# Layer 2 of a graph network: transposes alternating with the turned sums, and one product for both transposed halves

## The chip, the cores and the metric

The kernel runs on one core of a Trainium2 chip. A core has four compute engines used here: TensorE (PE, matrix products and transposes into PSUM; its weight loads are listed apart as PEld), VectorE (DVE), ScalarE (ACT) and GpSimd (POOL). Each works through its own queue in order, and semaphores make one wait for another. SyncE (SP) issues the loads from memory.

The metric is the device time of one execution in microseconds. The times before are 1147.15, 1148.13 and 1155.05 us, median 1148.13. The profile is of one execution, whose span from the first to the last instruction is 1148.0 us.

## What is computed

Four graph layers over the same 4096 nodes with 64 features and one sparse, weighted adjacency matrix of 4096 x 4096. Each layer normalizes x, works on it and adds its result to x. Layer 0 is a plain neighbour sum, layer 1 an attention with sigmoid weights, layer 3 weights each row's last 100 neighbours by powers of a half. The change is in layer 2, which sums logarithmic maps of all neighbours on the Poincare ball:

```python
def _logmap(x, y, c):
    sub = _mobius_add(-x, y, c)
    sub_norm = jnp.maximum(jnp.linalg.norm(sub, axis=-1, keepdims=True), MIN_NORM)
    ...
    arg = jnp.clip(sqrt_c * sub_norm, 0.0, TANH_CLIP)
    return 2.0 / (sqrt_c * lam_x) * jnp.arctanh(arg) * sub / sub_norm
...
deg = jnp.maximum(adj.sum(axis=1, keepdims=True), 1e-08)
w = adj / deg
log_ij = _logmap(x[:, None, :], x[None, :, :], c)
agg = jnp.einsum('ij,ijc->ic', w, log_ij)
transformed = agg @ weight + bias
origin = jnp.zeros_like(transformed)
return _expmap(origin, transformed, c)
```

So every pair of nodes gets a factor (an arctanh of a distance over its norm), the factor is multiplied by the adjacency, and the products weight a sum over source nodes. The factor of a pair is the same in both directions; the adjacency is not.

## The kernel before

**Blocks and groups.** Targets come in 8 blocks of 512 (`ib`), sources in groups of 256 (`g`, two column chunks of 128, `G = 2`). Layer 2 walks over `work`, a list of 72 entries `d`: block `ib` against the groups of the source blocks `J >= ib`, two groups (`half` 0 and 1) a block. Since the factor is symmetric, only `J >= ib` is computed. Where `J > ib` (`d["two"]`, 56 entries), the factors are used twice: as they are, for the targets of block `ib`, and transposed, for the targets of block `J`. On the diagonal there are a `first` entry, whose lower part is transposed once, and a `cut` entry.

**The steps of an entry.** Distances: fp32 and bf16 matmuls into a PSUM tile `mm` of 128x1024 (`l2_dists`, `l2_signs`). Then by turns ACT, POOL and DVE on 128x1024: `v<-mm` square on ACT, `v<-v` clamp on POOL (partly on DVE), logarithm `v<-v,minus` and root `t<-v` on ACT, `t<-mm,t` on DVE (`l2_coshs`), logarithm `t<-t` and inverse root `v<-v` on ACT, and `t<-t,v` on DVE (`l2_pairs`). The last is called the pairing here; `t` then holds the factors. From there two ways lead on:

- plain: DVE multiplies `t` by the adjacency tile (`l2_weights`, `w<-t,adj`), and PE sums with the sources' features `HA` as weights (`l2_sums`, `acc<-w,HA` with 512 moving columns, 65 weight columns);
- turned, for `two` only: PE transposes the eight 128x128 pieces of `t` into two PSUM banks, one per half `c` (`l2_turns`, `tr<-ident,t`); DVE multiplies each bank by the adjacency of the other direction (`l2_weights2`, `w<-tr,adj`, two instructions of 128x512) into `w2`; PE sums `w2` over its four chunks (`l2_sums2`, `acc<-w,HA` with 256 columns) into the accumulator `acc1`. After the second half of a source block, DVE (ACT for block 0) adds that accumulator to `others`, which frees it (`l2_gathers`).

An fp32 matmul shows as two passes in the trace, each with its own weight load, a transpose as one.

**What sets the order.** The order of each engine's queue is laid down when the program is built. Each stage is a generator that yields an engine and a time from which its next piece could run; `in_turn` always takes the piece that a small model (`Pace`) thinks can start first. `in_steps` ties generators to steps: in step k, PE issues the distances of entry k+1, the signs of entry k, the turned sums of entry k-2, the transposes of entry k-1, and the plain sums of entry k-1:

```python
(l2_dists(), -1, once), (l2_signs(), 0, once), (l2_sums2(), 2, if_two(1)),
(l2_turns(), 1, lambda d: 2 if d["two"] else 1), (l2_sums(), 1, once),
```

The two PSUM banks for transposes, `tr0` and `tr1`, are handed out by `bank()` from the list `spare` and given back by `emptied()`. They also serve the tail work of a finished block: `follow` queues generators such as `after2` (evicts the sums into `e`, transposes it, finishes the layer for the block) and `before3` (prepares layer 3). That work runs beside the next block's first steps. Where the model sees PE wait over 0.6 us, `keep_warm` puts in matmuls of the identity with itself (`tr<-ident`).

Of the kernel before, what the change touches and what calls it, by code (L numbers as in the profile page):

```python
# [9 lines left out]
F32 = mybir.dt.float32  # L10
# [6 lines left out]
PSUM = bass.MemoryType.PSUM  # L17

P = 128
D = 64  # L20
N = 4096
NC = N // P
W = 512
NB = N // W
CB = W // P
G = 2
# [36 lines left out]
class Pace:  # L63
# [11 lines left out]

    @staticmethod
    def name(ap):
        return getattr(getattr(ap, "tensor", ap), "name", None)

    def cost(self, engine, op, out, ins, rest, kw):  # L80
        n = per_partition(out)
# [61 lines left out]
def kernel(ctx: ExitStack, tc: tile.TileContext, a: dict, out: bass.AP):  # L143
# [4 lines left out]
    pace = Pace()  # L148
    PE, DVE, ACT, POOL = (
        InOrder(tc, e, pace, name)  # L150
        for e, name in (
            (nc.tensor, "PE"), (nc.vector, "DVE"), (nc.scalar, "ACT"), (nc.gpsimd, "POOL"),
        )
    )
# [5 lines left out]
    rows = ctx.enter_context(tc.tile_pool(name="rows", bufs=2))  # L160
    ps_mm = ctx.enter_context(tc.tile_pool(name="ps_mm", bufs=2, space=PSUM))
    ps_acc = ctx.enter_context(tc.tile_pool(name="ps_acc", bufs=1, space=PSUM))
    ps_tr = ctx.enter_context(tc.tile_pool(name="ps_tr", bufs=2, space=PSUM))


    x = keep.tile([P, NC, D], F32, name="x")
# [174 lines left out]
    in_use = []  # L341
    spare = [0, 1]

    def bank():
        k = spare.pop(0)
        t = ps_tr.tile([P, W], F32, tag=f"tr{k}", name="tr", bufs=1)
        in_use.append((t, k))
        return t

    def emptied(t):  # L350
        k = [k for k in in_use if k[0] is t][0]
        in_use.remove(k)
        spare.append(k[1])
# [379 lines left out]
    def latest(*times):  # L733
        return None if None in times else max(times)
# [86 lines left out]
    def ready(t, more=0.0):  # L821
        return pace.ready[pace.name(t)] + more
# [229 lines left out]
    def l2_dists():  # L1052
        for d in work:
            yield "PE", lambda: latest(
                l1[-1].get("dist"), rows_at.get((2, d["J"])), pair_tiles[-2].get("read")
            )
            pair_tile(d)
            ps = part(d, d["ps"])
            for c in range(G):
                b = slice(c * D, (c + 1) * D)  # L1060
                PE.matmul(
                    ps[:, c, :], LT[b, d["g"], :], RT[b, targets(d)], start=True, stop=False
                )
            for c in range(G):
                b = slice(2 * c * Q, (2 * c + 1) * Q)
                PE.matmul(
                    ps[:, c, :], LB[b, d["g"], :], RB[b, targets(d)], start=False, stop=True
                )
            d["dist"] = pace.latest
# [18 lines left out]
    def l2_clamps_v():  # L1088

        for d in work:  # L1090
            yield "DVE", lambda: d.get("square")
            if d["shared"]:
                v = d["v"].rearrange("p c i -> p (c i)")[:, 0:CLAMPED]
                DVE.tensor_scalar(v, v, FLOOR, None, ALU.max)
            d["clamped_v"] = pace.latest

    def l2_signs():
        for d in work:
            yield "PE", lambda: d.get("square")
            for c in range(G):  # L1100
                b = slice((2 * c + 1) * Q, (2 * c + 1) * Q + 2)
                PE.matmul(
                    part(d, d["ps"])[:, c, :], LB[b, d["g"], :], RB[b, targets(d)],
                    start=False, stop=True, skip_group_check=True,
                )
            d["signed"] = pace.latest
# [26 lines left out]
    def l2_coshs():  # L1133
        for d in work:
            yield "DVE", lambda: latest(d.get("root"), d.get("signed"))
            t = part(d, d["t"])
            DVE.scalar_tensor_tensor(t, part(d, d["ps"]), 0.5 * SC, t, ALU.max, ALU.add)
            d["read"] = pace.latest
# [22 lines left out]
            d["weighed"] = pace.latest  # L1161
            used(d)

    def l2_turns():
        for d in work:
            for c in range(G if d["two"] else 0):
                yield "PE", lambda: d.get("paired") if spare else None
                d["tr", c] = ps = bank()
                for k in range(CB):
                    b = slice(k * P, (k + 1) * P)  # L1170
                    PE.transpose(ps[:, b], d["t"][:, c, b], ident)
            if d["first"]:
                yield "PE", lambda: d.get("paired") if spare else None
                d["tr", 0] = ps = bank()
                for k in range(CB):
                    b, c = slice(OWN + k // G * P, OWN + (k // G + 1) * P), k % G
                    PE.transpose(ps[:, k * P : (k + 1) * P], d["t"][:, c, b], ident)
            d["turned"] = pace.latest
            if d["cut"]:
                yield "ANY", lambda: d.get("paired")  # L1180
                d["turned"] = d["paired"]
# [15 lines left out]
    def l2_weights2():  # L1197
        k = -1
        for n, d in enumerate(work):
            if d["first"]:  # L1200
                own = work[n + 1]
                yield "DVE", lambda: latest(
                    ready(d["tr", 0]) if ("tr", 0) in d else None, arrival(own),
                    ago(work, n + 1, 2, "summed"),
                )
                own["w"] = w2["pool"].tile([P, G, W], F32, tag="w", name="w")
                DVE.tensor_mul(
                    own["w"][:, :, 0:OWN], d["tr", 0].rearrange("p (k j) -> p k j", j=OWN),
                    own["adj"][:, :, 0:OWN],
                )  # L1210
                emptied(d["tr", 0])
                used(own)
            k += d["two"]
            for c in range(G if d["two"] else 0):
                yield "DVE", lambda: latest(
                    ready(d["tr", c]) if ("tr", c) in d else None,
                    ready(d["adj2"]) if "adj2" in d else None, ago(twos, k, 2, "summed2"),
                )
                if c == 0:
                    d["w2"] = w2["pool"].tile([P, CB, G * P], F32, tag="w2", name="w2")  # L1220
                j = (d["half"] * G + c) * P
                DVE.tensor_mul(
                    d["w2"][:, :, c * P : (c + 1) * P],
                    d["tr", c].rearrange("p (k j) -> p k j", j=P), d["adj2"][:, :, j : j + P],
                )
                emptied(d["tr", c])
            d["weighed2"] = pace.latest

    def l2_sums():
        for d in work:  # L1230
            yield "PE", lambda: latest(d.get("weighed"), take(0, d))
            if d["first"]:
                accs["l2"] = ps_acc.tile([P, W], F32, tag="acc0", name="acc")
                st["acc_free"][0] = None
            acc = accs["l2"]
            for c in range(G):
                PE.matmul(
                    acc[0 : D + 1, :], HA[:, d["g"] * G + c, :], d["w"][:, c, :],
                    start=(d["first"] and c == 0), stop=(d["last"] and c == G - 1),
                )  # L1240
            d["summed"] = pace.latest
            if d["last"]:
                ib = d["ib"]
                others = w2["others"][:, ws(ib)] if ib else None
                follow(
                    with_mark(3, ib, after2(ib, acc, others, st), before3(ib, None)),
                    ON_V if ib else ON_S, evicts=True,
                )

    def l2_sums2():  # L1250
        for d in twos:
            yield "PE", lambda: latest(
                d.get("weighed2"), 0.0 if d["half"] else st["acc_free"][1]
            )
            if d["half"] == 0:
                accs["turned"] = ps_acc.tile([P, W], F32, tag="acc1", name="acc")
                st["acc_free"][1] = None
            acc = accs["turned"][0 : D + 1, :]
            part = slice(d["half"] * G * P, (d["half"] + 1) * G * P)
            for k in range(CB):  # L1260
                PE.matmul(
                    acc[:, part], HA[:, d["ib"] * CB + k, :], d["w2"][:, k, :],
                    start=(k == 0), stop=(k == CB - 1),
                )
            d["summed2"] = pace.latest

    def l2_gathers():
        for d in twos:
# [25 lines left out]
    def if_two(n):  # L1294
        return lambda d: n if d["two"] else 0
# [174 lines left out]
    def l3_sum():  # L1470
# [22 lines left out]
        if d["last"]:  # L1493
# [5 lines left out]
        feed(order, "early"), feed(order23, "second"), second_tables(), second_part(), third_part(), l2_loads2(),  # L1499
        l0_sums(), l1_sums(), l1_weights(), l1_sigmoids(), l1_atts(),  # L1500
        in_steps(
            (l2_dists(), -1, once), (l2_signs(), 0, once), (l2_sums2(), 2, if_two(1)),
            (l2_turns(), 1, lambda d: 2 if d["two"] else 1), (l2_sums(), 1, once),
        ),
        in_steps(
            (l2_first_logs(), 0, once), (l2_roots(), 0, once), (l2_squares(), -1, once), (l2_inverses(), 0, once), (l2_logs(), 0, once),
# [1 line left out]
        l3_counts(),  # L1508
        in_steps(
            (l2_pairs(), 1, once), (l2_weights(), 1, once),  # L1510
            (l2_coshs(), 0, once), (l2_clamps_v(), -1, once), (l2_weights2(), 1, lambda d: 2 if d["two"] else 1 if d["first"] else 0),
        ),
        l2_clamps(), l2_gathers(), l3_weights(), l3_pass(), l3_masks(), l3_bias(),
        degree_sums(0, l0), degree_sums(1, l1), constants(), *later_constants(),
# [46 lines left out]
```

## Time and profile before

| | before |
|---|---|
| runs, us | 1147.15, 1148.13, 1155.05 |
| profiled execution, span, us | 1148.0 |
| mean granted TensorE clock | 0.990 |
| layer 2, about | 485 to 945 us of the span |
| `acc<-w,HA`, 256 columns, 500 to 900 us | 432 passes, 385 ns each |
| `tr<-ident,t` 128x128, 500 to 900 us | 456 transposes, 273 ns each |
| `w<-tr,adj` 128x512 | 120, 683 ns each |
| `t<-mm,t` 128x1024, 540 to 860 us | 48, 1220 ns each |

Nearly every instruction is recorded through one helper, so all have line L135 and are told apart by their tiles, as out<-in. Times are microseconds from the start of the span unless marked ns. Matmuls are pipelined: the 273 ns of a transpose is its whole way, while the next may start earlier, so for PE the distance from start to start counts. `xN` counts instructions (passes) in a merged line. "[0.30 <-DVE w]" behind a line means that the engine was idle for 0.30 us before it, and that DVE's write of `w` ended that. In the chain of waits every piece of work is followed back to what released it; what lies on it sets the end.

### The profile page before, as it was taken

How to read it: one execution, taken by the hardware profiler on the slowest of the kernel's cores; microseconds unless marked ns; L12 is line 12 of the kernel's file. 1: busy time of each engine (PE TensorE's matmuls, PEld its weight loads, DVE VectorE, ACT ScalarE, POOL GpSimd, SP SyncE). 2: the span in 40 equal slices, each digit the busy share in tenths (PEclk: the TensorE clock that was granted, in tenths of full speed). 3: DMA queues.
4: the chain of work that ended last, by engine and by line, in shares of the span. 5: the costliest groups of instructions: out<-in, count | busy, mean ns of one | idle time of the engine just before them, and what ended most of it. 6: DMA issues, size and time to landing. Idle time of an engine off the chain costs nothing.

```text
span 1148.0 us, 16026 instructions
## 1 busy us (share of the span) xinstructions
PE 1084.0 (94%) x5564; PEld 460.5 (40%) x5564; DVE 925.0 (81%) x1505; ACT 787.4 (69%) x1287; POOL 260.2 (23%) x150
## 2 busy tenths in 40 slices
PE   6889999999999999999999999999999879999998
PEld 3234443333333333345445445445444433333332
DVE  7689989869988888688989989899999994555550
ACT  1154546676776667889989889897988665555554
POOL 3021322112000000153343343343434300000000
PEclk9899999999999999999999999999999999999999
DMA  8899999865787677534535535435355499888930
GB/s 299 342 408 389 408 385 344 290 234 192 235 258 247 219 245 237 186 129 150 192 135 168 199 116 196 167 131 198 119 212 166 147 384 350 319 319 297 338 111 10
DMA packets 77194, 271.80 MB, mean 237 GB/s; under 512 B 10040, under 2 KB 11064, under 8 KB 77112
## 3 DMA queue, kind: packets, MB, share of 16 engines
q1 hardware_dynamic: 75456, 270.57, 65.9%
q8 instruction: 44, 0.72, 0.3%
q10 hardware_dynamic: 1656, 0.20, 0.1%
q14 instruction: 38, 0.31, 0.1%
HBM read 269.68 MB, written 1.05 MB: 236 GB/s over the span
## 4 chain that ended last, share of the span: by engine, by line
PE 51%; DVE 17%; issue 11%; ACT 9%; DMA 6%; POOL 6%; ACTq 0%; POOLq 0%; SPq 0%; DVEq 0%
PE acc L135 24%; PE mm L135 16%; PE tr L135 11%; DMA adj<-in_adjT_dram 5%; POOL v L135 5%; ACT wt L135 3%; DVE dg L135 3%; DVE sig L135 3%; DVE w L135 2%; DVE t L135 2%; ACT t L135 1%; ACT v L135 1%; ACT sig L135 1%; ACT lo_sq L135 1%; POOL lo_s L135 1%
## 5 line engine op out<-in xcount | busy, mean ns | idle before, releaser
L135 PE MATMUL acc<-w,HA 128*65 128x256 f32 (+1 forms) x736 | 246.1, 469 | 10.2 <-DVE w L135 10.0
L135 POOL TENSOR_SCALAR v<-v 128x1024 f32<-128x1024 f32 (+1 forms) x72 | 171.6, 2383 | 263.0 <-ACT v L135 263.0
L135 ACT ACTIVATE sig<-mm,att_b,att_a 128x1024 f32<-128x1024 f32 x128 | 148.6, 1201 | 51.0 <-PE mm L135 50.6
L135 ACT ACTIVATE wt<-mm 128x1024 uint16<-128x1024 f32 x124 | 120.2, 1020 | 87.2 <-PE mm L135 87.2
L135 DVE TENSOR_TENSOR sig<-sig,adj 128x1024 f32<-128x1024 f32 x128 | 152.6, 1220 | 30.0 <-ACT sig L135 26.7
L135 DVE TENSOR_TENSOR dg<-dg,adj 128x1024 f32<-128x1024 f32 x113 | 137.6, 1221 | 6.5 <-DMA adj<-in_adjT_dram 4.9
L135 PE MATMUL acc<-adj,HA 128*64 128x512 f32 x512 | 124.6, 615 | 13.0 <-DMA adj<-in_adjT_dram 12.6
L135 PEld LDWEIGHTS acc<-w,HA 128*65 128x65 f32 x736 | 94.1, 138 | 94.2 <-issue 50.0
L135 PE MATMUL mm<-qT,kT 64*128 64x512 f32 x512 | 129.2, 621 | 2.8 <-ACT sig L135 2.0
L135 PE MATMUL acc<-sig,HL 128*64 128x512 f32 x512 | 124.8, 608 | 1.7 <-DVE sig L135 1.5
L135 PE MATMUL acc<-wt,S 128*64 128x512 bf16 x496 | 100.0, 390 | 0.2 <-ACT wt L135 0.2
L135 ACT ACTIVATE v<-v,minus 128x1024 f32<-128x1024 f32 x72 | 79.1, 1099 | 29.8 <-POOL v L135 27.7
L135 DVE SCALAR_TENSOR_TENSOR t<-mm,t 128x1024 f32<-128x1024 f32 x72 | 83.5, 1160 | 13.6 <-PE mm L135 11.0
L135 DVE SCALAR_TENSOR_TENSOR t<-t,v 128x1024 f32<-128x1024 f32 x72 | 83.3, 1157 | 3.3 <-ACT t L135 2.7
L135 DVE TENSOR_TENSOR w<-t,adj 128x1024 f32<-128x1024 f32 x72 | 83.5, 1160 | 1.4
L135 DVE TENSOR_SCALAR RT<-adj 128x1024 bf16<-128x1024 f32 x74 | 50.4, 695 | 41.1 <-PE mm L135 39.9
L135 DVE TENSOR_TENSOR w<-tr,adj 128x512 f32<-128x512 f32 x120 | 77.5, 683 | 7.3 <-PE tr L135 7.2
L135 ACT ACTIVATE v<-mm 128x1024 f32<-128x1024 f32 x72 | 69.6, 967 | 14.4 <-PE mm L135 14.4
L135 ACT ACTIVATE t<-t 128x1024 f32<-128x1024 f32 x72 | 72.2, 1003 | 9.1 <-DVE t L135 9.0
L135 PE MATMUL mm<-RT,LT 64*128 64x512 f32 (+1 forms) x288 | 78.4, 621 | 0.0
L135 ACT ACTIVATE t<-v 128x1024 f32<-128x1024 f32 x72 | 72.7, 1010 | 2.1
L135 PEld LDWEIGHTS mm<-qT,kT 64*128 64x128 f32 x512 | 43.7, 186 | 71.1 <-issue 35.6
(215 smaller groups left out, 1411.3 us busy)
## 6 DMA issues: line engine op xcount, KB each, us to landing
adj<-in_adjT_dram SPq DMA_DIRECT2D x512, 512.0 KB, 4.7
x<-in_x_dram SPq DMA_DIRECT2D x4, 256.0 KB, 3.8
out_dram<-h SPq DMA_DIRECT2D x8, 128.0 KB, 2.5
b<-in_b_dram ACTq DMA_DIRECT2D x2, 32.0 KB, 5.6
W<-in_W_dram ACTq DMA_DIRECT2D x3, 16.0 KB, 4.8
W0T<-in_W0T_dram ACTq DMA_DIRECT2D x2, 16.0 KB, 5.5
W1T<-in_W1T_dram ACTq DMA_DIRECT2D x1, 16.0 KB
W1T<-in_b_dram ACTq DMA_DIRECT2D x1, 0.2 KB
```

Source lines behind the costliest of these rows:

```text
L135: done = self.tc.keep_in_program_order(getattr(self.engine, op)(*args, **kw))
```

## The change

`l2_turns` and `l2_sums2` become one generator, `l2_turns_and_sums2`. For entry n of `work` it issues the transposes of entry n and the turned sums of entry n-1 in two parts, one per half `c`. In a part, four turned matmuls (now 128 columns wide, for half `c` alone) and four transposes alternate one by one. A part starts when the pairing of entry n is done, bank `c` is spare, and `w2` of entry n-1 is ready (`weighed2`); the first part of a source block also needs `acc1` free. At ends of runs, where only one of the two kinds exists, the part holds that kind alone.

The two banks become one tile `trs` of two banks, allocated once, and bank `c` holds half `c` of a `two` entry; other users take the first spare one. `l2_weights2` then multiplies both halves in one instruction of 128x1024 when both are there, and gives both banks back behind it.

In the program as built, 224 turned matmuls of 256 columns become 448 of 128, 112 products `w<-tr,adj` become 56, and the count of `keep_warm` matmuls goes from 62 to 69 (in layer 2's blocks from the second on, from 7 together to 5 and, two steps later, 2). ScalarE's, POOL's and SyncE's instructions are the same in number.

```diff
-    ps_tr = ctx.enter_context(tc.tile_pool(name="ps_tr", bufs=2, space=PSUM))
+    ps_tr = ctx.enter_context(tc.tile_pool(name="ps_tr", bufs=1, space=PSUM))
+    trs = ps_tr.tile([P, 2, W], F32, name="tr")
...
-    def bank():
-        k = spare.pop(0)
-        t = ps_tr.tile([P, W], F32, tag=f"tr{k}", name="tr", bufs=1)
+    def bank(k=None):
+        k = spare[0] if k is None else k
+        spare.remove(k)
+        t = trs[:, k, :]
...
+    def turns_of(d):
+
+        for c in range(G if d["two"] else 1 if d["first"] else 0):
+            def start(c=c):
+                d["tr", c] = bank(c if d["two"] else None)
+
+            def one(k, c=c):
+                if d["two"]:
+                    src = d["t"][:, c, k * P : (k + 1) * P]
+                else:
+                    src = d["t"][:, k % G, OWN + k // G * P : OWN + (k // G + 1) * P]
+                PE.transpose(d["tr", c][:, k * P : (k + 1) * P], src, ident)
+
+            yield start, one
+
+    def sums2_of(d):
+
+        for c in range(G if d["two"] else 0):
+            def start(c=c):
+                if d["half"] == c == 0:
+                    accs["turned"] = ps_acc.tile([P, W], F32, tag="acc1", name="acc")
+                    st["acc_free"][1] = None
+
+            def one(k, c=c):
+                to = (d["half"] * G + c) * P
+                PE.matmul(
+                    accs["turned"][0 : D + 1, to : to + P], HA[:, d["ib"] * CB + k, :],
+                    d["w2"][:, k, c * P : (c + 1) * P], start=(k == 0), stop=(k == CB - 1),
+                    skip_group_check=True,
+                )
+
+            yield start, one
+
+    def steps_of(n):
+
+        turns = list(turns_of(work[n]))
+        sums2 = list(sums2_of(work[n - 1])) if n else []
+        return [(sums2[c : c + 1], turns[c : c + 1]) for c in range(max(len(turns), len(sums2)))]
+
+    def l2_turns_and_sums2():
+        for n, d in enumerate(work):
+            parts = steps_of(n)
+            old = work[n - 1] if n else None
+            for c, (sum2, turn) in enumerate(parts):
+                yield "PE", lambda: latest(
+                    *([d.get("paired") if (c in spare if d["two"] else spare) else None] if turn else []),
+                    *([old.get("weighed2"), 0.0 if c or old["half"] else st["acc_free"][1]] if sum2 else []),
+                    0.0,
+                )
+                for start, _ in sum2 + turn:
+                    start()
                 for k in range(CB):
...
+                    for _, one in sum2 + turn:
+                        one(k)
...
-            for c in range(G if d["two"] else 0):
+            if d["two"]:
                 yield "DVE", lambda: latest(
...
-                    d["w2"][:, :, c * P : (c + 1) * P],
-                    d["tr", c].rearrange("p (k j) -> p k j", j=P), d["adj2"][:, :, j : j + P],
-                )
-                emptied(d["tr", c])
+                    d["w2"].rearrange("p k (c j) -> p c k j", j=P),
+                    trs.rearrange("p c (k j) -> p c k j", j=P),
+                    d["adj2"][:, :, j : j + G * P].rearrange("p k (c j) -> p c k j", j=P),
+                )
+                for c in range(G):
+                    emptied(d["tr", c])
...
-            (l2_dists(), -1, once), (l2_signs(), 0, once), (l2_sums2(), 2, if_two(1)),
-            (l2_turns(), 1, lambda d: 2 if d["two"] else 1), (l2_sums(), 1, once),
+            (l2_dists(), -1, once), (l2_signs(), 0, once), 
+            (l2_turns_and_sums2(), 1, lambda d: len(steps_of(work.index(d))) + d["cut"]), (l2_sums(), 1, once),
```

More of the change, by code (lines that the diff above doesn't have):

```diff
@@ L77, in name @@
     def name(ap):
-        return getattr(getattr(ap, "tensor", ap), "name", None)
+        name = getattr(getattr(ap, "tensor", ap), "name", None)
+        if name is not None and name.startswith("tr_"):
+            return f"{name}_{ap.offset % (2 * W) // W}"
+        return name
     def cost(self, engine, op, out, ins, rest, kw):
@@ L1162, in l2_weights @@
             used(d)
-    def l2_turns():
-        for d in work:
-            for c in range(G if d["two"] else 0):
-                yield "PE", lambda: d.get("paired") if spare else None
-                d["tr", c] = ps = bank()
-                for k in range(CB):
[L1170 to L1177, printed above, removed]
+    def turns_of(d):
[9 more added lines that the diff above has]
+            yield start, one
@@ new lines, in steps_of @@
+    def steps_of(n):
[14 more added lines that the diff above has]
+                    start()
+                for k in range(CB):
+                    for _, one in sum2 + turn:
+                        one(k)
+            if old is not None and old["two"]:
+                old["summed2"] = pace.latest
@@ L1213, in l2_weights2 @@
             k += d["two"]
-            for c in range(G if d["two"] else 0):
+            if d["two"]:
                 yield "DVE", lambda: latest(
-                    ready(d["tr", c]) if ("tr", c) in d else None,
+                    *(ready(d["tr", c]) if ("tr", c) in d else None for c in range(G)),
                     ready(d["adj2"]) if "adj2" in d else None, ago(twos, k, 2, "summed2"),
                 )
-                if c == 0:
-                    d["w2"] = w2["pool"].tile([P, CB, G * P], F32, tag="w2", name="w2")
-                j = (d["half"] * G + c) * P
+                d["w2"] = w2["pool"].tile([P, CB, G * P], F32, tag="w2", name="w2")
+                j = d["half"] * G * P
                 DVE.tensor_mul(
-                    d["w2"][:, :, c * P : (c + 1) * P],
-                    d["tr", c].rearrange("p (k j) -> p k j", j=P), d["adj2"][:, :, j : j + P],
-                )
-                emptied(d["tr", c])
+                    d["w2"].rearrange("p k (c j) -> p c k j", j=P),
+                    trs.rearrange("p c (k j) -> p c k j", j=P),
+                    d["adj2"][:, :, j : j + G * P].rearrange("p k (c j) -> p c k j", j=P),
+                )
+                for c in range(G):
+                    emptied(d["tr", c])
             d["weighed2"] = pace.latest
@@ L1248, in l2_sums @@
                 )
[L1250 to L1253, printed above, removed]
-            )
[L1255 to L1265, printed above, removed]
     def l2_gathers():
@@ L1510 @@
             (l2_pairs(), 1, once), (l2_weights(), 1, once),
-            (l2_coshs(), 0, once), (l2_clamps_v(), -1, once), (l2_weights2(), 1, lambda d: 2 if d["two"] else 1 if d["first"] else 0),
+            (l2_coshs(), 0, once), (l2_clamps_v(), -1, once), (l2_weights2(), 1, lambda d: 1 if d["two"] or d["first"] else 0),
         ),
```

## The prediction

> **What bounds the kernel now.** I read the page first. Layer 2 runs from about 485 to 945 us of the span.
>
> ```profile
> PE 1084.0 (94%) x5564; PEld 460.5 (40%) x5564; DVE 925.0 (81%) x1505; ACT 787.4 (69%) x1287; POOL 260.2 (23%) x150
> ```
>
> TensorE is busy nearly everywhere, but that is a mean, so I cut layer 2 into windows (after the length: busy time of PE, PEld, DVE, ACT, POOL, then granted clock, DMA share, GB/s).
>
> ```profile
> 600.00:663.00 63.00, 62.70 (x312) 31.58 (x309) 60.59 (x72) 55.76 (x57) 25.34 (x13) 1.00 0.50 171
> 663.00:684.60 21.60, 19.53 (x92) 8.37 (x90) 18.75 (x36) 17.33 (x28) 9.35 (x5) 1.00 0.43 144
> 684.60:734.00 49.40, 49.38 (x245) 25.36 (x246) 47.49 (x56) 44.09 (x46) 19.18 (x10) 1.00 0.48 170
> ```
>
> Two kinds of stretch alternate. While a target block has groups with `two`, PE never rests (49.38 of 49.40 us) and DVE is 96% busy. Around the diagonal, where one target block ends and the next begins, PE has gaps of 2 us in 22 and waits pass between engines. The chain of waits says the same; its columns are start, length, work:
>
> ```profile
> 684.62 1.94 PE acc L135 x8
> 686.56 0.87 PE tr L135 x8
> 687.44 1.72 PE acc L135 x4
> 689.15 1.39 PE mm L135 x8
> 690.54 1.87 PE acc L135 x8
> ...
> 696.39 1.76 PE tr L135 x14
> ```
>
> One step is 1.87 (turned sums, 4 matmuls in 8 passes) + 0.87 (8 transposes) + 1.72 (plain sums) + 1.39 (distances) = 5.85 us. So in saturated stretches (63 + 49.4 + 38 + 26 + 16 us by the windows, 33 steps, and some 5 steps at the end of block 0) only PE's own streaming counts. The x14 are `keep_warm`'s matmuls: filler the planner put in where it believed PE idle, lying on the path.
>
> **Part 1, alternation on PE.** Eight passes of 256 columns become sixteen of 128 between the same eight transposes. From the timeline, 256-wide passes start 0.2155 us apart and transposes 0.109 (0.87/8). A 128-wide fp32 pass is not in this loop, but filler has that width and wider weights: 14 take 614.72 - 613.06 = 1.66 us, 0.119 each with the first load, 0.111 without. Low end 0.109: 16 x 0.109 - 8 x 0.2155 = +0.02 us a step. High end 0.119: +0.18. I take +0.02, since the transposes are the same width in the same place; over 38 steps +0.8 us, at most +7. Switching between transposes and matmuls is free where it occurs now: the last transpose to the first plain sum takes 0.109 as between two transposes, filler to turned sum 0.112. Could it be below nothing, that transposes wait for their weights (128 columns) and the sums' short loads (65) would hide them? These rows exclude it:
>
> ```profile
> 61.33 0.60 PE L135 MATMUL tr<-ident,HL 128*64 128x128 f32 x4 [2.41 <-DVE HL L135]
> ...
> 669.26 0.60 PE L135 MATMUL tr<-ident,t 128*128 128x128 f32 x4
> ```
>
> Half the weight columns, same 0.60 us: the stream sets the pace, not the load. [...]
>
> **Part 2, one product for both halves.** 112 products of 128x512 become 56 of 128x1024. The pair takes 1.29 us (below); one 128x1024 with a PSUM input takes 1.22 (t<-mm,t, mean 1220 ns). So 0.07 us is saved a pair, not 2 x 0.683 - 1.22 = 0.146, since the second starts before the first ends. In a saturated step it is hidden by PE. [...]
>
> What is late next: the product now waits for all eight transposes.
>
> ```profile
> 643.91 1.94 PE L135 MATMUL acc<-w,HA 128*65 128x256 f32 x8
> ...
> 646.33 1.29 DVE L135 TENSOR_TENSOR w<-tr,adj 128x512 f32<-128x512 f32 x2 [0.23 <-PE tr L135]
> ...
> 647.53 1.21 DVE L135 SCALAR_TENSOR_TENSOR t<-t,v 128x1024 f32<-128x1024 f32 x1
> ```
>
> It starts 0.44 us later (four transposes), at 646.78, and the pairing product t<-t,v behind it at about 647.92 instead of 647.53. Who waits: DVE's other work in the step, at start-to-start times of 1.14 (product) + 1.13 + 1.13 + 1.13, 0.4 to 0.8 of clamp and 0.60 of gather in every second step, is 5.0 to 5.9 of 5.85; DVE still comes round. PE needs the pairing at 649.76 and has it at 649.13. In steps with a gather (`others`, 0.68, after the pairing) the turned accumulator comes free at 649.73 where PE wants it at 649.76: cover is nearly gone, 0 to 0.1 us in some 14 steps. I take +0.3.
>
> **Part 3, a new wait.** The turned sums used to run while DVE finished the pairing; now PE's second instruction of the merged block is a transpose that waits for it, and all that follows on PE queues behind. In a saturated step it is ready (above). At the start of a target block it is not:
>
> ```profile
> 683.28 1.29 DVE L135 TENSOR_TENSOR w<-tr,adj 128x512 f32<-128x512 f32 x2
> ...
> 684.48 1.22 DVE L135 SCALAR_TENSOR_TENSOR t<-t,v 128x1024 f32<-128x1024 f32 x1
> 684.62 1.94 PE L135 MATMUL acc<-w,HA 128*65 128x256 f32 x8 [0.30 <-DVE w L135]
> ...
> 686.40 1.04 PE L135 MATMUL tr<-ident,t 128*128 128x128 f32 x8
> ```
>
> Pairing ends at 685.70; PE has done 0.2 us of sums by then and waits 0.85. The block ends at about 688.1, not 687.27: +0.83 us in each of four blocks. But the built order also moves filler there: of the 7 fillers two steps later, 5 now stand just before this block, inside the wait, and 2 remain. That takes 10 passes x 0.111 = 1.1 us off the path. Net -0.3 a block, -1.1 in all; with the filler not covered, +0.8 x 4 = +3.3. Block 0 gets 4 more fillers, 8 x 0.111 = +0.9; 8 more near the end lie where PE has gaps (51 busy of 62 us from 884 to 946): nothing.
>
> **Part 4, block ends.** After the last product the order on DVE was pairing, eviction `e`, weights `w`; it is now pairing, `w`, `e`.
>
> ```profile
> 664.65 1.21 DVE L135 SCALAR_TENSOR_TENSOR t<-t,v 128x1024 f32<-128x1024 f32 x1
> ...
> 665.78 0.68 DVE L135 TENSOR_TENSOR e<-acc,others 65x512 f32<-65x512 f32 x1
> 666.38 1.21 DVE L135 TENSOR_TENSOR w<-t,adj 128x1024 f32<-128x1024 f32 x1
> ...
> 666.87 0.46 PE L135 MATMUL tr<-ident,e 65*128 65x65 f32 x4
> ```
>
> Product at 663.90 (before 663.44), pairing 665.04, `w` 666.17, `e` 667.30 to 667.98: PE's transposes of `e` slip from 666.87 to 668.02, 1.15 us, and the signs and turned sums queue behind them. POOL's clamp at 668.09 and ScalarE's work up to 673 do not depend on it and hide part; by the same addition the next cosh moves from 675.18 to about 675.9. I take +0.7 in four blocks, +2.8; ends -0.2 (`w` is earlier) and +1.15, so -0.8 to +4.6. Where the product itself is on the chain (599.97, 683.28, twice more), -0.07 each: -0.3.
>
> **Sum.** +0.8 + 0.3 - 1.1 + 0.9 + 2.8 - 0.3 = +3.4 us against the profiled span of 1148.0; the median of the runs shown is 1148.1, with 0.1 around the span. Forecast 1151.5. All low ends (0.8, 0, -1.1, 0, -0.8, -0.6) give -1.7, all high ends (7, 1.4, 3.3, 1.6, 4.6, 0) +18; rarely all together. From 868 on the order changes in ways I did not follow, next to two waits on adjacency loads (3.95 and 5.01 us in the chain): another 3 us either way.
>
> **Rivals.**
> *Each alternation costs PE.* 56 steps x 16 changes between matmul and transpose. Where PE changes tile shape the trace shows 0.09 us (plain sum to distances, 0.522 instead of 0.429). At that price 38 x 16 x 0.093 = 57 us: 1205. It decides (over 1%) from 0.019 us a change. Against: the free changes above; for: a change hidden under a 256-wide pass has not been seen under 128. 0.10.
> *DVE becomes the bound.* If the product's four-dimensional pattern runs no faster than two, or clamps beside POOL take 0.8 each time, DVE's two steps need 11.8 us or more against 11.7 of PE, the gather comes late, and PE waits 0.1 to 0.4 us a step: +4 to +15 beside the sum, 1156 to 1166. For: 0.23 us of DVE slack a step; against: the addition in part 2. 0.15.
> *It is faster.* [...] 0.12, half of it over 1%.
> *It does not alternate.* The built order shows 448 turned matmuls of 128 columns one by one with transposes, so 0.01, at 1148.
>
> **How the numbers follow.** The forecast has 0.62. A measurement of this kernel tells 1% (11.5 us: under 1136.6, over 1159.6) from no change. Slower: 0.10 from the first rival, 0.08 from the second, 0.03 from the forecast's high ends: 0.21. Faster: 0.06. Same: 0.73. The range 1144 to 1164 holds the forecast, most of the second rival and half of the third.
>
> **What would show it.** In the profile after: acc<-w,HA 128x256 is gone and 128x128 passes stand 0.109 apart with tr between; PE in the long windows still without gaps; w<-tr,adj 128x1024 near 1.22 us; a PE wait on DVE t at block starts, under 1 us; `e` behind `w` and tr<-ident,e about 1.1 us later. The prediction is wrong if alternating passes stand further apart than 0.115, if PE waits in the middle of a block, or if the diagonal windows shrink.

## The result, and the profile after

The changed kernel takes 1187.8 us (median of 4 runs, 1184.0 to 1195.0), the kernel before, with one run more than in the table above, 1147.9. The ratio is 1.032, with a 95% interval of 1.027 to 1.037: slower by some 40 us. The prediction said 1151.5, within 1144 to 1164. The profiled execution, the slowest of the four, has a span of 1193.2 us, 45.2 more than before.

The page after, first its busy times, then the granted clock in 40 slices:

```profile
PE 1109.8 (93%) x6026; PEld 509.9 (43%) x6026; DVE 921.7 (77%) x1449; ACT 789.7 (66%) x1287; POOL 265.9 (22%) x150
...
PEclk9879999999999999999999999999999879999999
```

TensorE's busy time grew by 26 us, yet no share rose but that of the weight loads: the engines wait for each other more. Four slices have a granted clock of 0.7 or 0.8, two behind the start and two around the end of layer 2. Its mean is 0.970, against 0.990.

The saturated stretches that the prediction argued from are as they were. The windows that answer to those of before (same columns):

```profile
618.84:682.20 63.36, 62.56 (x395) 38.11 (x392) 57.76 (x61) 55.99 (x57) 26.36 (x13) 1.00 0.49 169
682.20:706.10 23.90, 20.38 (x106) 9.65 (x104) 19.57 (x34) 17.69 (x28) 9.31 (x5) 1.00 0.37 133
706.10:755.70 49.60, 49.07 (x310) 30.32 (x311) 45.24 (x47) 44.24 (x46) 20.19 (x9) 1.00 0.47 170
```

63.0, 21.6 and 49.4 us have become 63.4, 23.9 and 49.6. The long windows hardly moved; the one around the diagonal is 2.3 us longer, and TensorE sits idle for 3.5 us of it instead of 2.1.

To see where the rest goes I took ScalarE's square `v<-mm` of each entry as a mark, since both kernels have it 72 times in the same order. The mark of the first entry comes at 493.1 us instead of 476.6, the last at 937.0 instead of 902.8. So of the 45.2 us, **16.5 are lost before layer 2 has begun**, 17.7 in layer 2 and 11.0 behind it, although the diff edits layer 2's transposes. What layers 0, 1 and 3 share with layer 2 is the pair of transposition banks.

The view of TensorE's waits (released by: us in total, times, longest) names what is new. Before:

```profile
PE tr L135 <- DVE l L135: 1.4, 1, 1.4
...
PE tr L135 <- ACT qq L135: 1.0, 2, 0.6
...
PE tr L135 <- DVE e L135: 0.8, 1, 0.8
```

After:

```profile
PE tr L138 <- DVE total L138: 8.2, 8, 2.2
...
PE tr L138 <- DVE e L138: 4.4, 4, 1.2
PE tr L138 <- DVE l L138: 3.7, 5, 1.4
PE tr L138 <- ACT qq L138: 3.4, 3, 2.3
PE acc L138 <- DVE others L138: 3.1, 5, 1.2
```

`total` and `others` are not in the view of before at all. `qq` belongs to layer 1's tail work, `total` to layer 3's counts, `e` and `l` to the tail work at layer 2's block ends: all of it work that takes its bank with `bank()`. `others` is the gather, which comes up again under e4.

One such place in layer 1, from the timeline before:

```profile
127.36 1.16 PE L135 MATMUL tr<-WqkT,columns 65*128 65x128 f32 x8
...
128.36 0.33 PE L135 MATMUL tr<-W0T,e 128*128 128x64 f32 x2
...
128.56 0.59 ACT L135 COPY qkb<-tr 128x512 f32<-128x512 f32 x1 [1.52 <-PE tr L135]
```

and after:

```profile
135.07 1.16 PE L138 MATMUL tr<-WqkT,columns 65*128 65x128 f32 x8
...
136.06 0.33 PE L138 MATMUL tr<-W0T,e 128*128 128x64 f32 x2
...
137.57 0.33 PE L138 MATMUL tr<-ones_f,dg 128*128 128x1 f32 x2
...
137.94 0.59 ACT L138 COPY qkb<-tr 128x512 f32<-128x512 f32 x1 [3.20 <-PE tr L138]
...
138.56 0.16 DVE L138 COPY deg<-tr 128x4 f32<-128x4 f32 x1 [0.30 <-ACT qkb L138]
```

ScalarE copies `qkb` out of one bank, where `tr<-WqkT,columns` wrote it, 1.20 us behind that write's start before and 2.87 after. In between TensorE writes `tr<-W0T,e` and `tr<-ones_f,dg` into the *other* bank, and the copy now stands behind the last of these. The semaphore events of the trace say the same: the copy is released by the `ones_f,dg` matmul, which writes the bank that it does not read, where before it was released by `WqkT,columns` in its own bank. Three of the eight copies `qkb` are released so in the changed kernel (and in e1 and e7 below), and none before (nor in e2). Then VectorE's `deg<-tr`, from the second bank, waits for ScalarE's copy out of the first.

### The profile page after: what moved, and what is told of

Same layout as the page of the kernel before. It is cut to its first block, busy times and chain, and to the rows that moved or that the text cites. A ratio compares the mean times of both kernels' runs of the same rounds, so it can differ in the third digit from the quotient of the medians.

```text
span 1193.2 us, 16850 instructions
## 1 busy us (share of the span) xinstructions
PE 1109.8 (93%) x6026; PEld 509.9 (43%) x6026; DVE 921.7 (77%) x1449; ACT 789.7 (66%) x1287; POOL 265.9 (22%) x150
## 4 chain that ended last, share of the span: by engine, by line
PE 46%; issue 15%; ACT 13%; DVE 12%; POOL 10%; DMA 3%; ACTq 0%; POOLq 0%; SPq 0%; DVEq 0%
PE acc L138 21%; PE mm L138 15%; PE tr L138 10%; POOL v L138 8%; ACT wt L138 3%; DMA adj<-in_adjT_dram 3%; ACT v L138 2%; DVE dg L138 2%; DVE sig L138 2%; DVE t L138 1%; ACT lo_sq L138 1%; ACT t L138 1%; ACT sig L138 1%; DVE w L138 1%; DVE r_n L138 1%
## 5 line engine op out<-in xcount | busy, mean ns | idle before, releaser
L138 PE MATMUL acc<-w,HA 128*65 128x128 f32 (+1 forms) x1184 | 289.0, 359 | 10.5 <-DVE w L138 7.2
L138 PEld LDWEIGHTS acc<-w,HA 128*65 128x65 f32 x1184 | 149.7, 142 | 65.9 <-issue 49.9
L138 PE MATMUL acc<-adj,HA 128*64 128x512 f32 x512 | 130.2, 642 | 12.3 <-DMA adj<-in_adjT_dram 12.1
L138 PE MATMUL mm<-qT,kT 64*128 64x512 f32 x512 | 132.2, 634 | 2.5 <-ACT sig L138 2.0
L138 PE MATMUL tr<-ident,t 128*128 128x128 f32 x480 | 125.6, 279 | 6.1 <-DVE t L138 2.0
L138 DVE TENSOR_TENSOR w<-tr,adj 128x1024 f32<-128x1024 f32 (+1 forms) x64 | 73.9, 1155 | 27.2 <-PE tr L138 26.8
```

Of the source, the lines that this page charges most:

```text
L138: done = self.tc.keep_in_program_order(getattr(self.engine, op)(*args, **kw))
```

## The experiments

**Theory 1**: dependencies follow the tile. Since both banks are one tile, whoever reads or writes one bank waits for work on the other, in all layers; the double buffering is gone. **Theory 2**: the alternation, the later product or the new wait for the pairing costs the time. Beside the time, each run gives its mean granted clock. Time multiplied by clock varied little among the runs of one kernel (standard deviation 0.6 to 2.7 us, while the times themselves differed by up to 15), so it is shown as a rough measure of the time at a full clock; it takes idle stretches at half clock for a loss too. The runs lie in four sessions, not all on one chip, each with its own runs of the kernel before: the result's, e1 to e3, e4 to e7, and e8 with e9. Each ratio is to the kernel before of the same session.

| run | median us | ratio to before (95%) | time x clock, mean | layer 2's first and last mark, profiled |
|---|---|---|---|---|
| before, by session (4, 13, 7, 17 runs) | 1147.9, 1153.9, 1150.5, 1152.1 | | –, 1136.6, 1137.5, 1136.1 | 476.6, 902.8 |
| changed | 1187.8 | 1.032 (1.027-1.037) | 1159.2 | 493.1, 937.0 |
| e1 one tile only | 1172.1 | 1.016 (1.010-1.022) | 1149.5 | 492.5, 923.5 |
| e2 alternation, two tiles | 1158.9 | 1.004 (1.000-1.008) | 1140.6 | 484.5, 919.3 |
| e3 one tile in layer 2 | 1168.7 | 1.014 (1.009-1.019) | 1149.9 | 479.9, 922.5 |
| e4 the same, old order | 1167.1 | 1.016 (1.011-1.022) | 1149.7 | 475.4, 914.8 |
| e5 one tile, two products | 1179.9 | 1.027 (1.021-1.032) | 1159.6 | 483.1, 923.8 |
| e6 changed again | 1185.8 | 1.030 (1.024-1.035) | 1161.9 | 487.2, 931.1 |
| e7 one tile outside layer 2 | 1168.2 | 1.016 (1.012-1.019) | 1146.1 | 488.4, 915.8 |
| e8 before, gaps filled | 1151.0 | 0.998 (0.996-1.001) | 1139.5 | 477.3, 903.5 |
| e9 changed, gaps filled | 1185.4 | 1.028 (1.023-1.033) | 1163.8 | 481.4, 925.5 |

**e1: the kernel before with the one tile, and nothing else.**

```diff
-    ps_tr = ctx.enter_context(tc.tile_pool(name="ps_tr", bufs=2, space=PSUM))
+    ps_tr = ctx.enter_context(tc.tile_pool(name="ps_tr", bufs=1, space=PSUM))
+    trs = ps_tr.tile([P, 2, W], F32, name="tr")
...
-        t = ps_tr.tile([P, W], F32, tag=f"tr{k}", name="tr", bufs=1)
+        t = trs[:, k, :]
```

The planner still sees two banks, so every engine has the same instructions in the same order as before; the tile lies in the same two PSUM banks as the two tiles did.

> The kernel before with one edit: its two transposition banks become one tile of two banks; every engine's instructions and their order stay as before, only the waits between them change. Theory 1 (the one tile makes the work on one bank wait for the work on the other, in all layers): about 1180 to 1190 us, a half granted clock around 63 to 76 us as in the changed kernel, and layer 2's first square on ScalarE at about 493 us of the span instead of 477. Theory 2 (the alternation, the later product or the new wait for the pairing costs the time): 1148 us, first square at 477 us.

1172.1 us against 1153.9: the tile alone costs 18 us, where theory 2 had nothing. But it is only half of the loss; theory 1 as I had put it, the tile as the whole cause, is too simple. Layer 2's first mark is at 492.5 us as in the changed kernel, its steps cost just 4.8 us more than before, nearly all at block ends (7.40 instead of 6.51 us) and in steps with a gather (5.99 instead of 5.85).

**e2: the changed kernel with two tiles** (the allocation in e1's diff, turned round), and so with the product in halves.

```diff
-                DVE.tensor_mul(
-                    d["w2"].rearrange("p k (c j) -> p c k j", j=P),
-                    trs.rearrange("p c (k j) -> p c k j", j=P),
...
+                for c in range(G):
+                    DVE.tensor_mul(
+                        d["w2"][:, :, c * P : (c + 1) * P],
+                        d["tr", c].rearrange("p (k j) -> p k j", j=P),
+                        d["adj2"][:, :, j + c * P : j + (c + 1) * P],
+                    )
```

> The changed kernel with two separate tiles for the banks again and so the product in two halves of 128x512 one after the other; the alternation, the common generator and the new wait stay. Theory 1: 1147 to 1154 us, with layer 2's first square at 477 us. Theory 2: 1180 to 1188 us. A recorded prediction of 1151.5 us for the whole change would apply here, less 4 us of VectorE's time saved off the path.

1158.9 us, 4.9 above the kernel before: the alternation, the common generator and the new wait together cost 0 to 0.8%. The median lies above the range that I gave, and layer 2's first mark at 484.5 instead of 477, though the order and the waits ahead of it are those of before; 6.1 us of these 8 are a half clock, taken up under e8. At a full clock the 4.9 us are 4. Theory 2 falls as the main cause.

**e3: the changed kernel, the one tile only while layer 2 runs.** The bank function closes the pool and opens one with the other layout when no bank is in use.

```diff
+        if not in_use and trs["joint"] != ("second" in opened and "third" not in opened):
+            banks(not trs["joint"])
+        if trs["joint"]:
+            t = trs["one"][:, k, :]
+        else:
+            t = trs["of"].tile([P, W], F32, tag=f"tr{k}", name="tr", bufs=1)
```

> The changed kernel in its own order of instructions, but the one tile of two banks exists only while layer 2 runs; before and behind it two separate tiles serve. Theory 1, by stage: the 16.5 us that are lost ahead of layer 2 and the 11 us behind it come back, so 1160 us, with layer 2's first square at 477 us. Theory 2: within 5 us of the changed kernel's 1188, since layer 2 is unchanged.

1168.7, 15 us above the kernel before beside it, where the changed kernel was 40 above in its own session and 35 in that of e6: 20 to 25 us come back (I had expected 27), with the order unchanged on every engine. Theory 2 is excluded again. The rest, 15 us, arises in layer 2: its marks spread by 16.4 us more than before.

**e7: the reverse, the kernel before with the one tile in layers 0, 1 and 3 alone** (the condition of e3 turned round; order unchanged).

> The kernel before, order unchanged, with the one tile in layers 0, 1 and 3 alone. If the stages add up (the one tile throughout cost 18 us, of which layer 2's steps show 4.8): 1164 to 1168 us, layer 2's steps as in the kernel before (6.51 us at block ends, 5.85 in the middle). If the loss ahead of layer 2 was a clock that happened to be low in the profiled executions: 1154 us.

1168.2 us, 17.7 above the kernel before, and its layer 2 takes as long as before except for one step with a half clock (1.2 us). So all but 1.2 of the 17.7 us lie in stages in which the diff changes no line but the allocation. At a full clock 9 of the 17.7 are left (1146.1 against 1137.5); the rest comes with the lower clock. Behind layer 2 the span grew by 4.6 us, and the timeline shows why, six times over. One such place before:

```profile
1010.37 1.10 PE L135 MATMUL tr<-W,e 128*128 128x64 f32 x8
1010.49 0.69 DVE L135 CAST total<-tr 128x512 bf16<-128x512 f32 x1 [0.30 <-PE tr L135]
...
1011.31 0.59 PE L135 MATMUL tr<-total,spread 128*128 128x512 bf16 x2
```

and with the one tile:

```profile
1022.63 1.10 PE L138 MATMUL tr<-W,e 128*128 128x64 f32 x8
...
1023.78 0.69 DVE L138 CAST total<-tr 128x512 bf16<-128x512 f32 x1 [1.32 <-PE tr L138]
1024.52 0.59 PE L138 MATMUL tr<-total,spread 128*128 128x512 bf16 x2 [0.78 <-DVE total L138]
```

(These lines are the changed kernel's; e7 shows the same gap of 0.78 us six times, 4.7 us in all.) VectorE's `total` comes from one bank and could start when the counts are in, as it does before, 0.12 us behind the start of `tr<-W,e`; with the one tile it stands behind the end of `tr<-W,e`, which writes the other bank; TensorE waits 0.78 us for it.

**e5: the one tile throughout, but two products** (e2's edit on the changed kernel, tile kept). Order as in e2, so the pair e2 and e5 differs in waits alone.

> The changed kernel with one tile throughout, but its product in two halves; order as in the alternation with two tiles, so this run differs from that one in the waits alone. If the one tile alone costs what it cost without alternation (1172 against 1154), 1159 + 18 = 1177 us, and the rest to the changed kernel's 1188 belongs to the product of both halves and the order that it makes. If the alternation meets the one tile badly: 1185 us or more.

1179.9, between the two forecasts. That is 29.4 us above the kernel before of its session, where e2 was 4.9 above its own; at a full clock e5 is 19 above e2 (1159.6 against 1140.6), where the tile without the alternation cost 13 (e1: 1149.5 against 1136.6). So the tile costs more under the alternation. The product in one instruction, with the order it makes, is worth the remaining 6 us by the medians (1185.8 in e6), with intervals that overlap; by time multiplied by clock (1159.6 against 1159.2 and 1161.9) 0 to 2, so this part is not resolved by these runs.

**e4: which part of a block end is order, which is tile.** In layer 2's block ends of e3 the marks show 5.76 + 8.31 us (from the mark ahead to the marks of entries 44 and 45, counted from 0) where before had 5.22 + 6.51. e4 keeps e3's instructions, the product in one included, but charges the planner for it as for halves; every engine's order is then e2's, with `e` ahead of `w`.

```diff
-                    DVE.tensor_mul(
+                    tc.keep_in_program_order(nc.vector.tensor_mul(
...
+                    for c in range(G):
+                        pace.issue("DVE", "tensor_mul", (...), {})
```

> One tile in layer 2 only and the product of both halves at once, as in the run before it, but the planner is charged for the product as for two halves, which puts the eviction e ahead of the weights w again at block ends; every engine's order is then that of the alternation with two tiles. If the order on VectorE at block ends costs most of layer 2's loss (2.35 us a block there: a PE wait of 1.21 us for e, 0.34 us for l2<-tr), 4 block ends get 1.2 to 1.9 us each back: 1161 to 1164 us. If the waits between the banks cost it whatever the order is: 1167 to 1169 us.

1167.1 us, so my reading, order as the larger part, missed. Per block end the marks are

| | entry 44 | entry 45 |
|---|---|---|
| before | 5.22 | 6.51 |
| e2 | 5.26 | 6.52 |
| e4 | 5.76 | 7.54 |
| e3 | 5.76 | 8.31 |
| changed | 5.76 | 9.56, with a half clock; 8.31 at the end without one |

The order is worth 8.31 - 7.54 = 0.77 us here. The tile is worth 0.50 + 1.02, and the timeline of e4 shows both:

```profile
736.77 0.40 PE L138 MATMUL acc<-w,HA 128*65 128x128 f32 x2 [0.46 <-DVE others L138]
...
744.02 0.41 DVE L138 TENSOR_TENSOR l<-tr,Qc 128x256 f32<-128x256 f32 x1
744.36 0.68 DVE L138 SCALAR_TENSOR_TENSOR t<-mm,t 128x512 f32<-128x512 f32 x1
...
744.49 0.33 PE L138 MATMUL tr<-ident,t 128*128 128x128 f32 x1 [0.82 <-DVE l L138]
```

In the first line the product waited for all eight transposes (one tile again: e5, with the product in halves, has 5.83 there too), the pairing and the gather `others` behind it came later, and TensorE waits for the accumulator. In the last, transposes into bank 1 wait 0.82 us for VectorE to read `l2` (shown as `l`) out of bank 0. Why the order gained nothing in the end is only partly seen. The end of the fourth such block is 1.9 us longer in e4 (entry 63: 7.91 us, against 6.05 in e3). Even so e4's marks spread by 3.1 us less than e3's, 1.4 of it a half clock that only e3's profile has; but behind the last mark e4 takes 3.0 us more, and the cause of that stays open.

**e6: the changed kernel again**, beside e4, e5 and e7.

> The changed kernel itself, beside the other runs: 1184 to 1192 us by the runs so far. Time multiplied by the granted clock 1156 to 1162 us, where the kernel before gives 1133 to 1140 and the alternation with two tiles 1138 to 1142: if so, 23 us of the loss are there at a full clock and the rest is the throttle's.

1185.8 us, 35.4 above the kernel before there. At a full clock the difference is 1161.9 - 1137.5 = 24 us. Of these e2 explains 4 (1140.6 - 1136.6), e7 9 (1146.1 - 1137.5) and e3 beyond e2 9 (1149.9 - 1140.6), 22 together; the other 11 of the 35.4 us come with the lower clock. As the times stand, the same three make 4.9 + 17.7 + 9.8 = 32.4 us. In this run's profile 10.6 us are lost ahead of layer 2, 17.7 in it and 11.0 behind it; the first profile had 16.5, 17.7 and 11.0, and of its extra 5.9 us 4.7 lie in one stretch with a longer half clock (35.64 against 30.93 us, below).

**e8 and e9: the clock.** In the profiles the half clock comes in pieces of 3.41 us or a multiple (3.41 and 10.24 before; 3.41, 6.83 and 13.65 in the changed kernel), most of them behind a gap of TensorE (a few, such as those at 376.9 us before and at 390.5 and 462.2 in the changed kernel, behind gaps of only 0.3 to 0.6 us). In the changed kernel 2.33 us ahead of `tr<-ident,qq` at 147.25 us (0.64 before) are followed by 3.41 us at half from 148.2, and the gaps of 1.21 us at two of three block ends by as much at 762.6 and 827.4. What such a piece costs can be read without any run of its own, because before, e2, e3 and e4 have the same order and the same waits in layers 0 and 1. From the first `HL<-hb` on VectorE to the second copy `qkb<-tr` takes 27.79 us in before and e4, where the clock stayed full, and 33.89 in e2 and e3, where 13.65 us were at half: 6.1 us for one gap of 2.4 us that all four have. I put matmuls into that gap and two others, in both kernels:

```diff
+    def fill(n):
+        t = bank()
+        for _ in range(n):
+            tc.keep_in_program_order(nc.tensor.matmul(t[:, 0:P], ident, ident, start=True, stop=True))
+        emptied(t)
```

> The kernel before with three groups of eight identity matmuls (16 passes of 0.111 us, 1.8 us) put on TensorE into gaps of 2.26 to 2.42 us that are there: ahead of the first tr<-ident,HL (about 58 us), of the last tr<-twice,e (480 us) and of the first rank matmuls of layer 3 (943 us). If a gap of TensorE brings the half granted clock that begins 1 to 4 us behind it (3.4 to 13.7 us at a time in the profiles so far), those stretches vanish, the clock rises from 0.987 to 0.992 or more and the time falls by 4 to 6 us to about 1146 us; time multiplied by clock stays at 1137. If the two only happen to lie close together: 1150 to 1154 us and the same clock.

> The changed kernel with the same three groups. If the gaps bring the half clock: 1180 to 1183 us instead of 1186, time multiplied by clock still 1160 to 1162. It tells whether the new gaps of the one tile (2.32 us at 139 us, 1.2 us at block ends) keep their share: their half clocks should stay. If not: 1186 us.

In both profiles the gaps at 58 and 480 us are filled up to 0.3 to 0.4 us, and no half clock follows; the third group did not fill its gap, which stayed at 2.4 us in e8. With the gap at 480 us open, a half clock begins within 3 us of its end in all nine other profiles (0.5 us behind it before, 1.1 in the changed kernel); with the one at 58 us open, in seven of nine. The stretch named above takes 27.78 us in e8, and 29.59 in e9, where the changed kernel had 35.64 and 30.93 in its two profiles. So where a gap was filled its half clock did not come, and what stays, 29.59 - 27.78 = 1.8 us here, is the tile's own. The times that I had expected did not come, though, and by them alone the two would only happen to lie close together: 1151.0 against 1152.1, with an interval of -5 to +1 us, and 1185.4 against 1185.8 in e6. The highest of the kernel before's runs are missing (1154.6 is the highest of 12, where the 17 runs beside them reach 1162.4), the clock rose from 0.986 to 0.990, but time multiplied by clock rose as well by 3 us, which I cannot attribute. In e9 the new gaps from layer 2's block ends on kept their half clocks, seven pieces of 3.41 us from 751 us on; the new gap ahead of `tr<-ident,qq`, 2.32 us at 138 us, had none behind it this time, against what I had expected.

## Why the prediction was wrong

**The step that failed** is one that has no number: "The two banks become one tile" was described ahead of the prediction, and the prediction took from it only that both halves can be multiplied at once. The tail work that uses the banks one by one was left standing as if they were still two, and layers 0, 1 and 3 had no term in the sum at all. e7 prices this at 17.7 us outside layer 2 (9 at a full clock), e1 at 18 in all (13 at a full clock) with layer 2 in the old order. The lines to see it by were there: the chains of the tail work, where PE, ACT and DVE pass `tr` to each other, had only to be read with the question who else holds that tile.

**Part 1, alternation.** Right. The steady step after:

```profile
655.65 1.13 PE L138 MATMUL mm<-RT,LT 64*128 64x512 f32 x4
...
659.98 1.23 DVE L138 TENSOR_TENSOR w<-tr,adj 128x1024 f32<-128x1024 f32 x1 [0.52 <-PE tr L138]
...
661.59 1.13 PE L138 MATMUL mm<-RT,LT 64*128 64x512 f32 x4
```

661.59 - 655.65 = 5.94 us with a gather, 5.87 without, against 5.85 (+0.02 predicted). At full clock passes start 0.109 us apart at a change from sum to transpose, from transpose to sum, and without one. The rival of a cost per alternation is refuted, and so is the thought that the sums' short loads would hide the transposes' weights: no start comes earlier than the 0.109 us that transposes stood apart before.

**Part 2, the joint product.** Its length is as predicted (1.23 us in the steady step). What is late next was named correctly and sized wrongly: +0.3 us in all for the gather, where 0.07 us in each of six steps with a gather and 0.5 us at each of four block ends came, some 2.5 us. I had compared the gather with the sums in the steady step of 5.85 us; in the shorter one at the diagonal (5.22) TensorE arrives earlier, and the cover is gone. VectorE's busy time fell by 3.3 us (925.0 to 921.7), near the 56 x 0.07 = 3.9 that the saving a pair makes, and not 56 x 0.146 = 8.2: in the trace before, two products of 0.683 us take 1.29 us together, so the second starts before the first has ended.

**Part 3, the new wait.** About right: the step at a block start is 7.12 us against 7.11 (predicted -0.3). Block 0 was given +0.9 and lost 1.7 (1.2 in e2).

**Part 4, block ends.** The mechanism and the size were right at three of the four block ends: `e` goes behind `w`, TensorE waits 1.21 us for it (1.15 predicted), and the order is worth 0.77 us by the marks of e3 and e4 (0.7 predicted); at the fourth there is no such wait. But 0.50 + 1.02 us of waits across the banks are added at the same place, and a half clock in some:

```profile
762.00 0.46 PE L138 MATMUL tr<-ident,e 65*128 65x65 f32 x4 [1.21 <-DVE e L138]
...
762.91 0.42 DVE L138 TENSOR_TENSOR l<-tr,Qc 128x256 f32<-128x256 f32 x1
...
763.38 0.48 PE L138 MATMUL tr<-ident,t 128*128 128x128 f32 x1
...
763.65 0.64 PE L138 MATMUL acc<-w,HA 128*65 128x128 f32 x2
```

The first transpose of `t` starts behind the read of `tr` for `l`, and the two passes of the sum behind it take 0.64 us instead of 0.38: the half clock of 762.6 to 766.0.

**The sum.** e2 keeps of the prediction part 1, part 3 and block 0, which were given +0.8 - 1.1 + 0.9 = +0.6 us. It measured 4.9 (0.2 to 8.8 by its interval), 4 at a full clock. That e2 lies close to the +3.4 of the whole sum is chance: it has neither the joint product nor its order. The last eight steps of layer 2, where the fillers were put at nothing and the order was not followed, took 2.4 us more by e2's marks. What the sum left out is the one tile: 17.7 us outside layer 2 (e7), and 9.8 in it (e3 against e2, joint product and its order included, for which the sum had 2.8). With e2 these make 32.4 of the 33 to 40 us that the sessions show. Some 10 of these come with the clock, which goes down with the new gaps: 0.975 in the mean of the changed kernel's runs, 0.981 in e6 and 0.982 in e9, against 0.986 to 0.989. The exact share of the clock stays open: time multiplied by clock puts it at 11 us in the session of e6, but e8 shows that this product does not separate the two cleanly.

**The rival with VectorE as the bound** is not what happened: in the long windows VectorE's busy share fell from 96 to 91% (57.76 of 63.36 us) while TensorE's stayed at 99%. The prediction's own signs of being wrong did not speak. The passes stand 0.109 us apart, the diagonal windows grew where a shrinking was named, and in the middle of a block TensorE waits only in the steps with a gather, 0.07 us each. Most of the loss lay where no sign was set, outside layer 2.

## What to carry to other kernels

Two buffers that alternate were double buffering here only as long as the dependency tracking saw two (e1, with nothing but the one tile: 1172.1 us against 1153.9). Before merging tiles so that one instruction can span them, list everyone who uses either one, in all stages of the program, and ask of each what else is written or read in the other half meanwhile; here the merge saved a VectorE that was off the path some 3 us, and the one tile alone cost 19 at a full clock (e5 against e2) on the path that sets the end. When the allocation of a shared resource is edited, the sum needs a term for every stage that shares it, even where the diff leaves its lines alone.

A gap on TensorE had two prices here: its length, and the half clock that followed in some runs, 6.1 us behind the gap at 58 us (33.89 against 27.79).

## What the runs showed of the hardware

In these traces a half clock followed gaps of 1.21 us (at 762.6 and 827.4 us in the changed kernel). The pieces of half clock are 3.41 us long or a multiple, and came mostly behind gaps of 1.0 to 3.0 us, not each time: the gap at 58 us (2.41 us before, 2.85 in the changed kernel) was followed by 13.65 us at half in e1, e2 and e3, as in the changed kernel's first profile, by 10.24 in e7, by 3.41 in e5 and e6, by none in e4 and before. Where this gap and the one at 480 us were filled up to 0.3 to 0.4 us (e8, e9), none followed. The price can be read from the stretch named under e8. With two tiles it took 27.79 us at a full clock and 33.89 with 13.65 us at half; with the one tile in these layers it took 29.59 (e9), 30.93 with 3.41 us at half (e6), 33.94 with 10.24 (e7) and 35.64 with 13.65 (the changed kernel's first profile). At half clock the two passes of a 128-wide sum took 0.64 us instead of 0.38.

In the session of e8 the kernel before took 1147 to 1162 us from run to run with the same program. Where a few us are in question, the granted clock of each run belongs beside its time.
